# Longer edge and node-number loads, and residual rows turned on TensorE, in a graph attention kernel

## The chip, the cores and the metric

The kernel runs on one core of one Trainium2 chip. The metric is the device time of one execution in microseconds (us). A profile is one execution recorded by the hardware profiler; the span is the time from its first to its last instruction.

## What is computed

A graph has 6250 nodes with 128 features each and 206,250 edges, sorted by destination. With 8 heads of 16 features:

```python
Q, K, V = x @ WQ, x @ WK, x @ WV                        # 6250 x 128
Eh = edge_attr @ WE                                     # 206250 x 128
score = sum over a head of (K[src] * Q[dst] * Eh) / 4   # per edge and head
score = exp(clip(score, -5, 5))
h = segment_sum(V[src] * score, dst) / (segment_sum(score, dst) + 1e-6)
out = layernorm(x + h)
```

All inputs and the output are float32.

## The kernel before, in words

**Tiles and batches.** The edges are cut into 1612 tiles of 128 edges. Four tiles make a batch (the last few batches have two or one), 406 batches in all. Eleven tiles make a group; the edges of a group fall into a window of 128 destination nodes, and three groups cover a block of 128 nodes, with windows shifted by -43, 0 and 43.

**Start.** The transposed node features xT are loaded whole into SBUF (line 96) and stay there. TensorE makes the table of K and V from them (lines 227 to 246), which goes through a staging tile kvst with two buffers to HBM. Meanwhile GpSimd already gathers rows of x for the first 12 batches (XB), which are projected to K and V on the fly (project, lines 322 to 334). From batch 12 on, GpSimd gathers finished K and V rows from the table.

**One batch.** GpSimd issues one indirect gather for each tile (line 311), 128 rows of 1 KB, into a tile kvrows of a pool with GB = 16 buffers. Behind each batch from the twelfth on it executes an iota into a tile that nobody reads (line 319). From batch LOCK = 20 on, the first gather of batch b depends on the expansion of batch b-2 (line 314): the matmul of line 353, which spreads the rows of Q (loaded by load_q, line 278, in windows of 42 nodes in three bf16 parts) over the edges with a one-hot matrix. VectorE builds that matrix, onehotT (line 343), from node numbers relative to the window; these are held in HBM (relD, written by from_window, line 164) and loaded by load_rel (line 285), broadcast to 126 partitions, for RC = 16 tiles at a time in two buffers. TensorE multiplies the edge features by WE (line 357), from loads of CH = 8 tiles (line 295, load_chunk) in EB = 6 buffers. VectorE multiplies the expanded Q by that product (line 364), TensorE turns the result (turn, line 372), VectorE multiplies by the gathered K (stage_b, line 378) and sums per head (line 381), ScalarE takes the exponential (lines 390 and 392), VectorE forms the messages (line 412), and TensorE sums them per window with a one-hot matrix (stage_c, line 430).

**Finishing a block.** ScalarE copies each finished window to SBUF (line 440). When all windows of a block of 128 nodes are there, finish (line 403) adds them up on TensorE with shift matrices, ScalarE copies the sum (line 407), and a layernorm is made in small steps of VectorE between the batches' work (lines 595 to 620). It adds the block's rows of x, which stage_c has had loaded on SP's queue (load_x, line 591), and its result is stored on the same queue (line 620). The last group of all has its windows added straight into its PSUM tile.

**What sets the order.** Up to batch 12 a scheduler of the framework orders the instructions; from then on the order is that in which the loop over batches (line 463) writes them. SP's queue issues, in this order per batch: a store of a finished block, the edge load, the node numbers, the window of Q, and later the rows of Q just computed (line 266). An instruction at the head of a queue that waits holds up all behind it. In the loop, load_chunk(c + 3) is called when the batches of edge load c begin, load_rel one load ahead, load_q three windows ahead. After the loop, a general path runs if the edges were not sorted as assumed (line 521); here it is skipped.

Of the kernel before, what the change touches and what calls it, by code (L numbers as in the profile page):

```python
# [8 lines left out]
F32 = mybir.dt.float32  # L9
# [3 lines left out]
ALU = mybir.AluOpType  # L13
AX = mybir.AxisListType

P = 128
N, E, D, H, DH = 6250, 206250, 128, 8, 16
# [4 lines left out]
LEFT, RIGHT = 43, 128  # L22
XC = LEFT + N + RIGHT
OFF = (-43, 0, 43)
MW = D + H
B = 4
CH = 8
GB = 16
XB = 12
LOCK = XB + 8  # L30
STEP = 2
# [1 line left out]
HEAD = 132  # L33
NG = (NT + G - 1) // G
AHEAD = 2
EB = 6
SLAG = 2
WT = 8
RC = 16
NJ = (NT + WT - 1) // WT  # L40
QW = 42
QP = 3
# [38 lines left out]
def edge_attention(ctx: ExitStack, tc: tile.TileContext, x, xT, srcT, dstT, dstB, dst0, bnd, lo, eaT,  # L81
                   wq, wkv, we, out, kv, qtab, qs, relD):
    nc = tc.nc
# [8 lines left out]
    xT_sb = cp.tile([P, XC], F32, name="xT_sb")  # L92
# [19 lines left out]
    with ExitStack() as fast:  # L112
# [11 lines left out]
        ident = shift[:, P:2 * P]  # L124
# [78 lines left out]

        gp = fast.enter_context(tc.tile_pool(name="gather", bufs=GB))
        ep = fast.enter_context(tc.tile_pool(name="edges", bufs=EB))
        wp = fast.enter_context(tc.tile_pool(name="work", bufs=3))
        sp = fast.enter_context(tc.tile_pool(name="sums", bufs=7))
# [3 lines left out]
        psT = fast.enter_context(tc.tile_pool(name="psT", bufs=1, space=bass.MemoryType.PSUM))  # L211
# [36 lines left out]
        batches = cut_batches()  # L248
        nbat = len(batches)
        manual = []  # L250
        xbs, stores, norms, pending, ready = {}, [], [], [], []


        built, loaded, regs, rels = [], {}, [], {}
# [25 lines left out]
        def load_rel(c):  # L280
            if c in rels or c * RC >= NT:
# [3 lines left out]
            nc.sync.dma_start(rels[c][:, :n], relD.rearrange("j e -> (j e)")[None, c * RC * P:c * RC * P + n]  # L285
                              .to_broadcast([QROWS, n]))

        chunks, aggs, sums, st8, expanded = {}, {}, {}, {}, {}

        def load_chunk(c):  # L290
            if c in chunks or c * CH >= NT:
                return
            n = min(CH, NT - c * CH) * P
            tl = ep.tile([P, CH * P], F32, name="ea")
            nc.sync.dma_start(tl[:, :n], eaT[:, c * CH * P:c * CH * P + n])
            chunks[c] = tl

        def ea_tiles(t, n):

            load_chunk(t // CH)  # L300
            j = t % CH * P
            return chunks[t // CH][:, j:j + n * P]
# [92 lines left out]
        def add_windows(ps, q, stop):  # L395

            parts = [(k, k[0] * P + offset(*k) - q * P)
                     for k in ((q - 1, 2), (q, 0), (q, 1), (q, 2), (q + 1, 0)) if k in sums]
            for i, (k, s) in enumerate(parts):
                nc.tensor.matmul(ps, shift[:, P - s:2 * P - s], sums[k],  # L400
                                 start=i == 0, stop=stop and i == len(parts) - 1)

        def finish(q):
            ps = psT.tile([P, MW], F32, name="finps", tag="oT")
            add_windows(ps, q, True)
            fin = sp.tile([P, MW], F32, name="fin", bufs=2)
            nc.scalar.copy(fin, ps)
            pending.append(layernorm(nc, sp, fin, xbs.pop(q), out, q, stores))

        def messages(b):  # L410
            n, g, oh, m = st8[b]
# [5 lines left out]
        def stage_c(b):  # L417
            n, g, oh, m = st8.pop(b)
            for i in range(n):
                t = batches[b][i]  # L420
                k = group_of(t)
                if k[1] == 0 and k[0] not in xbs:
                    xbs[k[0]] = load_x(nc, sp, x, k[0])
                first, final = k not in aggs, k == group_of(NT - 1)
                if first:
                    aggs[k] = psA.tile([P, MW], F32, name="agg")
                    if final:
                        add_windows(aggs[k], k[0], False)
                last = t == NT - 1 or group_of(t + 1) != k
                nc.tensor.matmul(aggs[k], oh[:, i, :], m[:, i, :],  # L430
                                 start=first and not final, stop=last)
                if last and final:
                    norms.extend(pending)
                    pending.clear()
                    while norms:
                        fill()
                    norms.append(layernorm(nc, sp, aggs.pop(k), xbs.pop(k[0]), out, k[0], stores))
                elif last:
                    tl = sp.tile([P, MW], F32, name="sum")
                    nc.scalar.copy(tl, aggs.pop(k))  # L440
                    sums[k] = tl
                    if k[1] == 0 and k[0] > 0:
                        ready.append(k[0] - 1)
# [19 lines left out]
        for b in range(nbat + 4):  # L463
            if b >= XB and not manual:
                manual.append(fast.enter_context(tc.manual_schedule()))
            held += [(b + SLAG, store) for store in stores]
            stores.clear()
            if held and (held[0][0] <= b or b >= nbat):
                held.pop(0)[1]()
            if b < nbat:  # L470
                load_chunk(batches[b][0] // CH + EB - 3)
                load_rel(batches[b][0] // RC + 1)
                load_q(batches[b][0] // WT + QLOOK)
                g = gathered.pop(b) if b in gathered else gather(b)
                if b == min(XB, nbat - 1):
                    late_loads()
                if b == min(XB + 8, nbat - 1):
                    relative(C0, NT)
                if b == 14:
                    from_window(1)  # L480
                if b == 0:
                    for i in range(AHEAD):
                        stage_0(i)
                if b > 0:
                    turn(b - 1)
                stage_a(b, g)
            elif b == nbat:
                turn(b - 1)
            norms.extend(pending)
            pending.clear()  # L490
            for q in ready:
                finish(q)
            ready.clear()
            if 0 <= b - 2 < nbat:
                stage_b(b - 2)
            if 0 <= b - 3 < nbat:
                messages(b - 3)
            fill()
            if b + AHEAD < nbat:
                stage_0(b + AHEAD)  # L500
            if b < nbat:
                pairs(b)
            if 0 <= b - 2 < nbat:
                weigh(b - 2)
            if 0 <= b - 3 < nbat:
                stage_c(b - 3)
            fill()
            if b < nbat:
                while len(built) < q_built(min(NJ - 1, batches[b][0] // WT + QLOOK + 2)):
                    q_rows(len(built))  # L510
            if b == min(60, nbat):
                count_inside()
            if b == min(80, nbat + 1):
                inside = nc.values_load(cnt_i[0:1, 0:1], min_val=0, max_val=2 * EPAD,
                                        skip_runtime_bounds_check_because="two counts of EPAD edges")
# [72 lines left out]
def load_x(nc, sp, x, q):  # L588
    n = min(P, N - q * P)
    xb = sp.tile([P, D], F32, name="xb", bufs=3)  # L590
    nc.sync.dma_start(xb[:n], x[q * P:q * P + n])
    return xb


def layernorm(nc, sp, agg, xb, out, q, stores):

    n = min(P, N - q * P)
    def new(name, w, bufs=2):
        return sp.tile([P, w], F32, name=name, bufs=bufs)
    rz, h, st, mv, v, y, vh, w = (new(k, f) for k, f in (  # L600
        ("rz", H), ("h", D), ("st", 6), ("mv", 2), ("v", 1), ("y", 1), ("vh", 1), ("w", 1)))
    vec = nc.vector
    yield vec.tensor_scalar(rz[:n], agg[:n, D:], 1e-6, None, op0=ALU.add)
    yield vec.reciprocal(rz[:n], rz[:n])
    yield vec.tensor_tensor(h[:n].rearrange("p (h d) -> p h d", h=H),
                            agg[:n, :D].rearrange("p (h d) -> p h d", h=H),
                            rz[:n, :, None].to_broadcast([n, H, DH]), op=ALU.mult)
    yield vec.tensor_tensor(h[:n], h[:n], xb[:n], op=ALU.add)
    yield vec.bn_stats(st[:n], h[:n])
    yield vec.bn_aggr(mv[:n], st[:n])  # L610

    yield vec.tensor_scalar(v[:n], mv[:n, 1:2], 1e-5, None, op0=ALU.add)
    yield vec.tensor_scalar(y[:n].bitcast(I32), v[:n].bitcast(I32), -0.5, float(0x5F3759DF),
                            op0=ALU.mult, op1=ALU.add)
    yield vec.tensor_scalar(vh[:n], v[:n], -0.5, None, op0=ALU.mult)
    for _ in range(3):
        yield vec.scalar_tensor_tensor(w[:n], y[:n], vh[:n], y[:n], op0=ALU.mult, op1=ALU.mult)
        yield vec.scalar_tensor_tensor(y[:n], w[:n], 1.5, y[:n], op0=ALU.add, op1=ALU.mult)
    yield vec.tensor_scalar(h[:n], h[:n], mv[:n, 0:1], y[:n], op0=ALU.subtract, op1=ALU.mult)
    stores.append(lambda: nc.sync.dma_start(out[q * P:q * P + n], h[:n]))  # L620
# [46 lines left out]
```

## Time and profile before

| | |
|---|---|
| runs | 2202.32, 2204.58 and 2208.21 us, median 2204.58 |
| the profiled execution's own time | 2208.21 us |
| its span | 2206.3 us |
| mean granted TensorE clock | 0.866 |
| busy: POOL, DVE, PE, ACT | 1719.4, 1626.8, 1468.0, 478.9 us |
| moved by DMA | 398.18 MB, 180 GB/s on the mean |
| requests: edges (512 KB), node numbers (504 KB), residual rows (64 KB) | 202, 101 and 49 |

In the profile PE is TensorE, DVE is VectorE, ACT is ScalarE, POOL is GpSimd and SP the engine that issues most transfers; a q behind a name is the engine's queue of instructions. L311 is line 311. The page gives busy times, then groups of instructions with their mean in ns and the idle time before them with what ended it. A timeline row has the start and the duration in us, the instruction, and in brackets the idle time before it and its releaser. A row of waits has the total in us, the number of times and the longest. A row of windows has the stretch and its length, the busy time of PE, PE's weight loads, DVE, ACT and POOL with counts, the granted clock, the busy share of the DMA engines and GB/s.

### The profile page before, as it was taken

The numbers are of one execution on the slowest core, as the hardware profiler recorded it, in microseconds if no ns is written. First come the engines' busy times: TensorE is split into PE (matmuls) and PEld (weight loads), VectorE is DVE, ScalarE is ACT, GpSimd is POOL, SyncE is SP. The second block draws the span as 40 slices with busy tenths as digits, with TensorE's granted clock in tenths as the row PEclk, the third lists the DMA queues.
The fourth block names the chain that finished last, engine by engine and source line by source line (L and its number), as shares of the span: only waits on it lengthen the run. The fifth ranks groups of instructions, "written<-read, shape, count | busy, mean of one in ns | idle before, by whom it ended". The sixth has DMA issues, their size and how long they took to land.

```text
span 2206.3 us, 25324 instructions
## 1 busy us (share of the span) xinstructions
PE 1468.0 (67%) x6880; PEld 1026.4 (47%) x6880; DVE 1626.8 (74%) x3779; ACT 478.9 (22%) x1572; POOL 1719.4 (78%) x2013
## 2 busy tenths in 40 slices
PE   6976666676666666666666666666766666666665
PEld 4754444454444444444444444444444444444443
DVE  3797778677777777777776776777777777777776
ACT  2522222222222221222221221222222211221211
POOL 7737777877777787787777778778778777777876
PEclk9998888878888998888888898998898888887888
DMA  8746555665566556555666556556655566656552
GB/s 283 247 135 203 173 183 160 192 193 163 171 188 193 180 163 199 177 182 161 181 188 181 181 168 201 179 163 191 186 181 163 177 192 181 181 165 200 176 161 78
DMA packets 178486, 398.18 MB, mean 180 GB/s; under 512 B 61757, under 2 KB 87527, under 8 KB 178337
## 3 DMA queue, kind: packets, MB, share of 16 engines
q0 software_dynamic: 76592, 208.18, 31.8%
q1 hardware_dynamic: 100604, 187.38, 27.2%
q8 instruction: 57, 0.93, 0.2%
q10 hardware_dynamic: 1140, 0.93, 0.1%
q14 instruction: 93, 0.75, 0.1%
HBM read 381.54 MB, written 14.81 MB: 180 GB/s over the span
## 4 chain that ended last, share of the span: by engine, by line
POOL 42%; DMA 21%; DVE 15%; issue 14%; PE 7%; POOLq 0%; ACT 0%; DVEq 0%; ACTq 0%; SPq 0%
POOL kvrows L311 39%; DMA kvrows<-kv,src 20%; POOL pause L319 4%; DVE kq L378 4%; DVE sc L381 3%; PE agg L430 2%; DVE msg L412 2%; DVE onehot L339 2%; PE eps L357 2%; DVE onehotT L343 1%; PE kvps L333 1%; PE pps L372 1%; DVE eq L364 1%; DMA kv<-kvst 1%; DVE sc L384 1%
## 5 line engine op out<-in xcount | busy, mean ns | idle before, releaser
L311 POOL DMA_INDIRECT kvrows<-kv,src x1564 | 1487.1, 951 | 453.1 <-issue 384.8
L430 PE MATMUL agg<-msg,onehot 128*128 128x136 f32 x3224 | 542.5, 318 | 605.0 <-DVE msg L412 295.4
L430 PEld LDWEIGHTS agg<-msg,onehot 128*128 128x128 f32 x3224 | 479.3, 218 | 916.7 <-issue 768.9
L378 DVE TENSOR_TENSOR kq<-kvrows,pps 128x512 f32<-128x512 f32 x406 | 276.3, 680 | 472.6 <-DMA kvrows<-kv,src 468.5
L357 PE MATMUL eps<-ea,we_sb 128*128 128x512 f32 (+1 forms) x812 | 487.9, 686 | 0.7 <-ACT kvrows L334 0.7
L372 PE MATMUL pps<-shift,eq 128*128 128x128 f32 x1612 | 310.2, 324 | 98.3 <-DVE eq L364 85.9
L355 ACT COPY qT<-qps 128x512 f32<-128x512 f32 x406 | 236.7, 583 | 587.1 <-PE qps L353 586.8
L372 PEld LDWEIGHTS pps<-shift,eq 128*128 128x128 f32 x1612 | 214.2, 163 | 155.8 <-DVE eq L364 150.0
L364 DVE TENSOR_TENSOR eq<-qT,eps 128x512 f32<-128x512 f32 x406 | 272.4, 671 | 18.9 <-PE eps L357 16.2
L381 DVE TENSOR_REDUCE sc<-kq 128x32 f32<-128x512 f32 x406 | 276.0, 680 | 7.3
L390 ACT ACTIVATE bank<-sc 128x32 f32<-128x32 f32 x406 | 81.8, 201 | 918.5 <-DVE onehot L339 911.8
L412 DVE TENSOR_TENSOR msg<-kvrows,bank 128x512 f32<-128x512 f32 x406 | 274.5, 676 | 5.6 <-ACT bank L390 5.5
L339 DVE TENSOR_TENSOR onehot<-bank,dst_sb 128x512 f32<-128x512 f32 x406 | 275.4, 679 | 0.0
L357 PEld LDWEIGHTS eps<-ea,we_sb 128*128 128x128 f32 x812 | 186.4, 231 | 31.6 <-ACT kvrows L334 3.2
L343 DVE TENSOR_SCALAR onehotT<-relb,node 126x512 bf16<-126x512 bf16 x406 | 192.7, 476 | 6.4 <-DMA relb<-relD 5.7
L319 POOL IOTA pause<- 128x384 int32 x394 | 185.3, 470 | 2.9
L353 PE MATMUL qps<-onehotT,qw 126*128 126x512 bf16 x406 | 183.2, 451 | 0.7 <-ACT qT L355 0.7
L384 DVE TENSOR_SCALAR sc<-sc 128x32 f32<-128x32 f32 x406 | 89.0, 219 | 7.3
L392 ACT ACTIVATE msg<-sc 128x32 f32<-128x32 f32 x406 | 86.5, 213 | 0.0
L400 PEld LDWEIGHTS finps<-sum,shift 128*128 128x128 f32 x478 | 64.5, 195 | 26.1 <-issue 25.9
L400 PE MATMUL finps<-sum,shift 128*128 128x136 f32 x478 | 64.4, 282 | 0.0
L311 POOL DMA_INDIRECT kvrows<-x,src x48 | 46.0, 958 | 16.2 <-issue 14.0
(67 smaller groups left out, 528.5 us busy)
## 6 DMA issues: line engine op xcount, KB each, us to landing
ea<-eaT SPq DMA_DIRECT2D x201, 512.0 KB
relb<-relD SPq DMA_DIRECT2D x100, 504.0 KB
kvrows<-kv,src POOLq DMA_INDIRECT x1564, 2.8
qw<-qs SPq DMA_DIRECT2D x202, 31.5 KB
kv<-kvst SPq DMA_DIRECT2D x12, 512.0 KB
qs<-qst SPq DMA_DIRECT2D x48, 96.0 KB
xb<-x SPq DMA_DIRECT2D x48, 64.0 KB
out<-h SPq DMA_DIRECT2D x48, 64.0 KB
```

What stands on the lines that cost most here:

```text
L311: ins = nc.gpsimd.indirect_dma_start(out=g[:k, i, :f], out_offset=None, in_=rows, in_offset=bass.IndirectOffsetOnAxis(ap=src_col(t)[:k], a ...
L319: nc.gpsimd.iota(pause, pattern=[[1, 3 * P]], base=0, channel_multiplier=0)
L339: nc.vector.tensor_tensor(oh[:, :n], iota_p[:, None, :].to_broadcast([P, n, P]), rel[:, t0:t0 + n, None].to_broadcast([P, n, P]), op=ALU.i ...
L343: nc.vector.tensor_scalar(ohT[:, :n * P], rels[t0 // RC][:, e0:e0 + n * P], node[:QROWS], None, op0=ALU.is_equal)
L355: nc.scalar.copy(qT[:, :n * P], pq[:, :n * P])
L357: nc.tensor.matmul(pe[:, :n * P], we_sb, ea_tiles(t0, n), start=True, stop=True)
L364: nc.vector.tensor_tensor(eq[:, :n * P], qT[:, :n * P], pe[:, :n * P], op=ALU.mult)
L372: nc.tensor.transpose(pp[:, i, :], eq[:, i * P:i * P + P], ident)
L378: nc.vector.tensor_tensor(t1[:, :n], g[:, :n, :D], pp[:, :n], op=ALU.mult)
L381: nc.vector.tensor_reduce(sc[:, :n], t1[:, :n].rearrange("p b (h d) -> p b h d", h=H), axis=AX.X, op=ALU.add)
L412: nc.vector.tensor_tensor(m[:, :n, :D].rearrange("p b (h d) -> p b h d", h=H), g[:, :n, D:].rearrange("p b (h d) -> p b h d", h=H), exp_p[ ...
L430: nc.tensor.matmul(aggs[k], oh[:, i, :], m[:, i, :], start=first and not final, stop=last)
```

## The change

Edge loads hold CH = 16 tiles instead of 8 (1 MB instead of 512 KB), in EB = 3 buffers instead of 6, and load_chunk is called two loads ahead. Node-number loads hold RC = 32 tiles instead of 16 (1008 KB instead of 504 KB), still in two buffers, which takes 8 KB more per partition; the gather pool has GB = 13 buffers instead of 16, which gives 12 KB back. The loads of residual rows go. In their place TensorE turns 128 columns of xT into rows with an identity matrix, beside the window sums in the same PSUM tile, and ScalarE copies both together; for the last group there is a PSUM tile and a copy of its own. The iota behind each batch, the tie to the expansion two batches back, XB and LOCK are the same in both kernels.

```diff
-CH = 8
-GB = 16
+CH = 16
+GB = 13
...
-EB = 6
+EB = 3
...
-RC = 16
+RC = 32
...
-        xbs, stores, norms, pending, ready = {}, [], [], [], []
+        stores, norms, pending, ready = [], [], [], []
...
+        last_x = {}
...
+        def own_rows(ps, q):
+
+            nc.tensor.transpose(ps, xT_sb[:, LEFT + q * P:LEFT + q * P + P], ident)
+
         def finish(q):
-            ps = psT.tile([P, MW], F32, name="finps", tag="oT")
-            add_windows(ps, q, True)
-            fin = sp.tile([P, MW], F32, name="fin", bufs=2)
+            ps = psT.tile([P, MW + D], F32, name="finps", tag="oT")
+            own_rows(ps[:, MW:], q)
+            add_windows(ps[:, :MW], q, True)
+            fin = sp.tile([P, MW + D], F32, name="fin", bufs=2)
             nc.scalar.copy(fin, ps)
-            pending.append(layernorm(nc, sp, fin, xbs.pop(q), out, q, stores))
+            pending.append(layernorm(nc, sp, fin, fin[:, MW:], out, q, stores))
...
-                if k[1] == 0 and k[0] not in xbs:
-                    xbs[k[0]] = load_x(nc, sp, x, k[0])
                 first, final = k not in aggs, k == group_of(NT - 1)
                 if first:
                     aggs[k] = psA.tile([P, MW], F32, name="agg")
                     if final:
+                        px = psT.tile([P, D], F32, name="xps", tag="oT")
+                        own_rows(px, k[0])
+                        xb = last_x.setdefault(0, sp.tile([P, D], F32, name="xb", bufs=1))
+                        nc.scalar.copy(xb, px)
                         add_windows(aggs[k], k[0], False)
...
-                    norms.append(layernorm(nc, sp, aggs.pop(k), xbs.pop(k[0]), out, k[0], stores))
+                    norms.append(layernorm(nc, sp, aggs.pop(k), last_x[0], out, k[0], stores))
...
-                load_chunk(batches[b][0] // CH + EB - 3)
+                load_chunk(batches[b][0] // CH + 2)
...
-    yield vec.tensor_scalar(rz[:n], agg[:n, D:], 1e-6, None, op0=ALU.add)
+    yield vec.tensor_scalar(rz[:n], agg[:n, D:MW], 1e-6, None, op0=ALU.add)
```

## The prediction

> **What bounds the kernel now.** I read the busy times of the page first, then GpSimd's groups, then GpSimd's own timeline, because the busiest engine by share (POOL, 78%) looks as if it had 22% to spare.
>
> ```profile
> PE 1468.0 (67%) x6880; PEld 1026.4 (47%) x6880; DVE 1626.8 (74%) x3779; ACT 478.9 (22%) x1572; POOL 1719.4 (78%) x2013
> ...
> L311 POOL DMA_INDIRECT kvrows<-kv,src x1564 | 1487.1, 951 | 453.1 <-issue 384.8
> ...
> L319 POOL IOTA pause<- 128x384 int32 x394 | 185.3, 470 | 2.9
> ```
>
> The idle column shows that most of what is missing is "issue": a fixed gap behind every gather, not a wait. The timeline of GpSimd shows one batch:
>
> ```profile
> 1002.88 0.47 POOL L319 IOTA pause<- 128x384 int32 x1
> 1003.51 0.95 POOL L311 DMA_INDIRECT kvrows<-kv,src  x1 [0.16 <-issue]
> 1004.76 0.95 POOL L311 DMA_INDIRECT kvrows<-kv,src  x1 [0.30 <-issue]
> ...
> 1008.23 0.54 POOL L319 IOTA pause<- 128x384 int32 x1
> ```
>
> Four gathers of 0.951, three gaps of 0.30, the iota of 0.47 and gaps of 0.01 and 0.16 make 5.34 us. From one batch's first gather to the next, 380 full batches of four tiles take 5.357 us on the mean, 5.34 in the median: GpSimd runs nearly without a hole. The early timeline of the same engine has the one hole that matters:
>
> ```profile
> 106.13 0.47 POOL L319 IOTA pause<- 128x384 int32 x1
> 139.53 0.95 POOL L311 DMA_INDIRECT kvrows<-kv,src  x1 [32.94 <-DVE sc L384]
> ```
>
> This is batch 20, the first that is tied to an expansion of Q (line 314; LOCK is 20). The releaser that is named is wrong: the expansion of batch 18 on TensorE (line 353) starts at 138.63 and takes 0.63, and 0.27 later the gather starts. So the time is a sum of three: 139.53 until batch 20 may start, then 386 batches of gathers to the end of the last one at 2191.67 (2052.1 us), then 14.6 us of tail to 2206.3. An edit counts only if it moves the release of batch 20, GpSimd's rate, or the tail.
>
> **How much room the tie leaves afterwards.** For each batch b, I took the start of its first gather less the start of ScalarE's copy of the expansion of b-2 (line 355), which follows that expansion at once. It is 0.24 us for batch 20 and 2.07 for 21, then grows; from batch 30 on its median is 14.1 us and its least 7.0 (batch 63, behind the counting of batch 60). So GpSimd never waits for the rest of the core, though the rest waits for it:
>
> ```profile
> DVE kq L378 <- DMA kvrows<-kv,src: 468.5, 243, 6.2
> ...
> POOL kvrows L311 <- DVE sc L384: 37.7, 26, 32.9
> ...
> DVE onehotT L343 <- DMA relb<-relD: 5.7, 3, 3.8
> ```
>
> The 468.5 us are VectorE waiting for rows that GpSimd has yet to ask for or that are landing; they are no time to be won. Loads of node numbers were late three times in all, at the start.
>
> **What limits the first 139.5 us.** The windows show a stage of DMA, then TensorE, then VectorE:
>
> ```profile
> 16.00:50.00 34.00, 25.80 (x104) 19.52 (x102) 13.09 (x36) 10.39 (x31) 25.57 (x28) 0.91 0.90 291
> 50.00:65.00 15.00, 10.61 (x36) 6.65 (x37) 8.50 (x14) 5.79 (x12) 11.49 (x12) 0.81 0.85 256
> 65.00:113.00 48.00, 47.95 (x257) 36.34 (x256) 35.26 (x67) 24.87 (x62) 33.13 (x39) 0.99 0.72 224
> 113.00:139.50 26.50, 19.43 (x100) 13.98 (x99) 25.47 (x61) 6.26 (x22) 0.00 (x0) 0.91 0.31 94
> 139.50:2191.70 2052.20, 1352.16 (x6350) 941.24 (x6349) 1532.00 (x3548) 427.52 (x1434) 1637.95 (x1918) 0.86 0.59 178
> ```
>
> From 65 to 113 PE is busy 47.95 of 48, from 113 to 139.5 DVE 25.47 of 26.5: a shift that arrives at 65 goes through to the release. Before that, the table of K and V waits for its own stores (2.82 us at 37.07), which share the queue with the first loads:
>
> ```profile
> 29.27 0.42 SPq L285 DMA_DIRECT2D relb<-relD  x1
> ...
> 37.07 0.65 ACT L238 COPY kvst<-kvacc 128x256 f32<-128x256 f32 x2 [2.82 <-DMA kv<-kvst]
> ...
> 60.03 0.88 DVE L343 TENSOR_SCALAR onehotT<-relb,node 126x512 bf16<-126x512 bf16 x3 [3.79 <-DMA relb<-relD]
> ...
> 62.90 0.47 PE L326 MATMUL xtps<-shift,kvrows 128*128 128x128 f32 x1 [2.39 <-ACT xgT L328]
> ```
>
> **The change, part by part.** Its own execution is 2208.21 us with a span of 2206.3; the median of the runs is 2204.58, and shifts are added to either alike.
>
> 1. Doubled loads at the start: three stand before the last table stores (edge loads at 16.00 and 41.69, node numbers at 29.27). Each gains 504 to 512 KB. At the 291 GB/s of the window 16 to 50, that is 1.75 us each, 5.2 for three: the upper end. The lower end is 0: the stores may slip in between. I take the node numbers whole (1.75; a store issued 0.5 us behind them is the one waited for) and each edge load at 0.55, since 4 to 5 us pass between it and the next store: +2.9.
> 2. The second load of node numbers now is needed at batch 8, not at batch 4. So VectorE's 3.79 at 60.03 go. Behind them TensorE is late for 2.39; what is late next is the projection of the second batch (line 333), so I take the smaller: -2.4, between 0 and -3.8.
> 3. Own rows: 48 transposes in finish and one in the last group. A 128x128 transpose is 0.32 us by the mean of line 372. ScalarE's copy of a finished window takes 0.27 with 136 columns; a copy of 512 (line 355) takes 0.59, so 128 columns more are some 0.11. In the steady part both lie under GpSimd, at ScalarE 22% and PE 67% busy. If that cover were gone, they would cost 49 x (0.32 + 0.11), 21 us. In the VectorE stage before 139.5 there is one finish, 0 to +0.4: I take 0, as VectorE is then at work on the second window of node numbers.
> 4. The 49 loads of residual rows go from SP's queue. Nothing waits for them in the waits; 0.
> 5. Steady loads: the same bytes (less 3 MB of 398) in half as many requests. Edge loads are now asked for two loads ahead (at least 8 batches, 43 us) instead of three short ones (6 batches, 32 us), node numbers at least 6 batches ahead instead of 2. With 3 buffers an edge load waits for the last use of the third last one, and what stands behind it in SP's queue (node numbers, Q's rows, stores) waits too, for about one batch, 5.4 us; Q's rows are asked for 6 batches ahead, 32 us. 0.
> 6. 13 gather buffers: batches 13 to 19 now wait for messages of batches 0 to 6. Those end at 64.3, 71.1, 75.1, 79.3, 85.4, 89.9 and 95.3; the gathers start at 69.35 and every 5.34 us up to 101.42. All are free, by 3.6 us at the least, and a delay would fall into the 32.94 us hole. Later a buffer is 13 batches old, 70 us. 0.
> 7. Tail: one transpose and one copy on the final window's way, +0.2 (0 to +0.6, the transpose with a copy of 0.27).
> 8. GpSimd's rate: its instructions are the same, in the same order. Its holes (5.357 against a least of 5.33, over 386 batches) are 10 us in all; why single gathers are slow is not shown. I take 0, between -10 and +5.
>
> Sum: 2.9 - 2.4 + 0.2 = +0.7, 2208.9 beside the profiled execution and 2205.3 beside the median.
>
> Of the Trainium skill, "DMA: Bandwidth & Descriptors", section "Rules for kernel authors", asks for 1 MiB per DMA, and its fixed cost of about 2 us would, as an estimate for some 200 requests fewer, promise 400 us; the waits above show that nobody stands behind these requests, so I count none of it. The same page, "Queues, rings and completion order", speaks against the change: an engine alternates between queues packet by packet, so longer rows could hold up the gathers' packets; that would be the second rival.
>
> **Rivals.**
> - *The start gets longer* (same side of the bound): item 1 whole, item 2 worth nothing: 5.2 + 0.4 + 0.6 = +6.2, 2210.8. For it: DMA share 0.90 in the window. Against it: the 3.79 us stall is plainly a node-number load. Chance 0.14, a third of it above the bound.
> - *Gathers come too late* (slower): where an edge load and node numbers go out together, 2 MB stand on the queues where 1 MB did. By 291 GB/s that is 3.5 us more. VectorE's product began 1.83 to 9.26 us after a batch's last gather from batch 25 on. The tie bites when a batch is late by more than the room of 7.0 to 14.1 us. If every meeting (51) overshot by 1 us, +51: 2256. Against it: 3.5 is half of the least room. Chance 0.04.
> - *The holes close* (faster): half requests, fewer disturbances of GpSimd: -10 and item 2: 2192. For it: 16 of the periods exceed 5.45 us. Against it: of the 33 gathers over 0.975 us after 130, 19 have no SP request within 1.5 us. Chance 0.07.
> - The change does not do what it says, SP being held elsewhere: no time differs, 2204.6; within the forecast.
>
> **Numbers.** Forecast 2205.3, chance 0.75, its own range 2200 to 2210 (ends of items 1, 2 and 7, with the 2 to 4 us by which the shown runs differ). The whole range takes in the start's rival and a part of the closed holes: 2198 to 2213. The bound of 0.3% is 6.6 us, about what a measurement of this kernel can tell from no change. Faster 0.07, same 0.84, slower 0.09 (0.05 from the start, 0.04 from late gathers).
>
> **What would show it.** In the profile after: GpSimd's periods stay at 5.34 to 5.36; batch 20 starts between 136 and 145; no onehotT waits near 60; the copy into kvst near 37 waits about 2 us longer; the tail stays within a microsecond of 14.6; xb vanishes from the DMA issues. I am wrong if GpSimd waits again after batch 25, if its gathers or gaps change their length, or if the release moves by more than 6 us.

## The result, and the profile after

The changed kernel takes 2221.58 us in the median of 4 runs (2220.18 to 2223.96), the kernel before 2204.11 (2202.32 to 2208.21, 4 runs): ratio 1.0078, 95% interval 1.006 to 1.0095. It is slower by 17.5 us where 0.7 was forecast, and outside the forecast range. Of the runs below, one execution of e1_order took 3532.39 us and is left out of its median.

The profiled execution took 2221.16 us, span 2219.3 (2206.3 before). The prediction's sum of three splits the 13.0 us; the other 4.5 of the median's 17.5 are that the profiled run of before lies 4.1 above its median and that of the changed kernel 0.4 below its own. The release is the start of batch 20's first gather.

| part of the span | before | after | difference | forecast |
|---|---|---|---|---|
| until batch 20 is released | 139.53 | 155.17 | +15.6 | +0.5 |
| from there to the end of the last gather | 2052.1 | 2048.5 | -3.6 | 0 |
| tail | 14.6 | 15.6 | +1.0 | +0.2 |

The page of the changed kernel, in the columns that the prediction read, shows the long part unchanged:

```profile
PE 1456.2 (66%) x6929; PEld 1018.7 (46%) x6929; DVE 1608.3 (72%) x3779; ACT 483.1 (22%) x1573; POOL 1715.5 (77%) x2013
...
L312 POOL DMA_INDIRECT kvrows<-kv,src x1564 | 1482.4, 948 | 469.0 <-issue 379.8
...
L320 POOL IOTA pause<- 128x384 int32 x394 | 185.4, 471 | 2.7
```

A gather takes 948 ns for 951, and the 49 transposes show only as TensorE's count, 6929 for 6880. GpSimd's timeline has the loss, in the same hole as before:

```profile
106.94 0.47 POOL L320 IOTA pause<- 128x384 int32 x1
155.17 0.94 POOL L312 DMA_INDIRECT kvrows<-kv,src  x1 [47.76 <-PE qps L354]
```

47.76 us of idle where the prediction's row has 32.94. What was late in front of it is in the waits of the changed kernel (engine, instruction, releaser: us in all, times, longest):

```profile
DVE kq L379 <- DMA kvrows<-kv,src: 459.0, 168, 8.0
...
POOL kvrows L312 <- PE qps L354: 48.6, 6, 47.8
...
DVE wq L161 <- DMA dB_sb<-dstB: 9.2, 1, 9.2
...
PE eps L358 <- DMA ea<-eaT: 3.9, 1, 3.9
DVE onehotT L344 <- DMA relb<-relD: 2.6, 1, 2.6
```

The last three of these rows name loads that SP issues. The first two of them stand in no row of before, and each occurs **once**: against 459 us of harmless waiting for rows they look like nothing, but they lie ahead of the release, where every microsecond counts.

**The late second half of the destinations (9.2).** VectorE's part of the timeline, about batch 14:

```profile
132.79 0.15 DVE L161 TENSOR_TENSOR wq<-dB_sb,bnd_c 74x1 f32<-74x1 int32 x1 [9.25 <-DMA dB_sb<-dstB]
```

and before, where it did not wait:

```profile
117.30 0.15 DVE L161 TENSOR_TENSOR wq<-dB_sb,bnd_c 74x1 f32<-74x1 int32 x1
```

from_window(1), called at batch 14, turns that half into node numbers. Its load (line 158, 296 KB) is issued by SP, whose timeline reads:

```profile
107.56 0.35 SPq L278 DMA_DIRECT2D qw<-qs  x1
116.63 0.34 SPq L296 DMA_DIRECT2D ea<-eaT  x1
117.17 0.35 SPq L278 DMA_DIRECT2D qw<-qs  x1
117.56 0.37 SPq L189 DMA_DIRECT2D src<-srcT  x1
117.97 0.43 SPq L190 DMA_DIRECT2D dst_sb<-dstT  x1
118.59 0.35 SPq L278 DMA_DIRECT2D qw<-qs  x1
118.99 0.27 SPq L158 DMA_DIRECT2D dB_sb<-dstB  x1
```

and before:

```profile
107.48 0.27 SPq L158 DMA_DIRECT2D dB_sb<-dstB  x1
```

SP issues nothing from 107.9 to 116.63: the edge load there is to go into the oldest of three buffers, which batch 11 still reads. Behind it the queue bursts out: 1 MB of edges, two loads of 740 KB, and last the one that VectorE needs. It goes out at 118.99, 11.5 us later than in the kernel before, and VectorE has it at 132.79. Its place behind that burst costs too: its 74 packets of 4 KB run from 124.96, when the 740 KB loads are nearly through, to 132.39, 13.4 us after its issue; before, the last 4 KB packet ends at 116.41, 8.9 us after its issue. So its last packet comes 16.0 us later, 11.5 by the issue and 4.5 by the longer time from there. The copy of Q's expansion (qT) of batch 15 follows that of batch 14 by 18.1 us:

```profile
124.51 0.58 ACT L356 COPY qT<-qps 128x512 f32<-128x512 f32 x1 [0.80 <-PE qps L354]
...
142.64 0.58 ACT L356 COPY qT<-qps 128x512 f32<-128x512 f32 x1 [2.51 <-PE qps L354]
```

Before, by 8.3, so the difference is +9.8:

```profile
118.34 0.59 ACT L355 COPY qT<-qps 128x512 f32<-128x512 f32 x1 [0.80 <-PE qps L353]
...
126.67 0.59 ACT L355 COPY qT<-qps 128x512 f32<-128x512 f32 x1 [2.04 <-PE qps L353]
```

**Edge load 1 (3.9).** TensorE at batch 4:

```profile
82.10 1.10 PE L358 MATMUL eps<-ea,we_sb 128*128 128x512 f32 x2 [3.92 <-DMA ea<-eaT]
```

At batch 0 the loop asks for load 0 // 16 + 2 = 2. Load 1 (tiles 16 to 31, batches 4 to 7) is asked for by nobody until it is used: SP issues it at 73.24, with loads 0, 2 and 3 in the three buffers, after batch 3 lets load 0's buffer go. Before, six short buffers absorbed such a skip.

The start before that went nearly as forecast: the stall at 60 us is gone, the copy into kvst waits longer, and VectorE waits for the first node numbers:

```profile
39.17 1.34 DVE L344 TENSOR_SCALAR onehotT<-relb,node 126x512 bf16<-126x512 bf16 x4 [2.62 <-DMA relb<-relD]
40.66 0.65 ACT L238 COPY kvst<-kvacc 128x256 f32<-128x256 f32 x2 [4.44 <-DMA kv<-kvst]
```

VectorE's product kq, by batch, carries the sum: batch 3 at 77.6 (76.2 before: +1.4), batch 4 at 87.7 (82.2: +5.5, edge load 1 between them), batch 10 at 114.6 (108.4: +6.2); then the 9.8; the release comes at +15.6.

### The profile page after: what moved, and what is told of

It reads as the page before. It is cut to its first block, busy times and chain, and to the rows that moved or that the text cites. A ratio compares the mean times of both kernels' runs of the same rounds, so it can differ in the third digit from the quotient of the medians.

```text
span 2219.3 us, 25016 instructions
## 1 busy us (share of the span) xinstructions
PE 1456.2 (66%) x6929; PEld 1018.7 (46%) x6929; DVE 1608.3 (72%) x3779; ACT 483.1 (22%) x1573; POOL 1715.5 (77%) x2013
## 4 chain that ended last, share of the span: by engine, by line
POOL 27%; DMA 24%; DVE 21%; issue 14%; PE 8%; ACT 1%; DVEq 0%; POOLq 0%; ACTq 0%
POOL kvrows L312 25%; DMA kvrows<-kv,src 24%; DVE kq L379 5%; DVE sc L382 5%; PE agg L438 4%; DVE msg L418 3%; POOL pause L320 2%; PE eps L358 2%; DVE eq L365 2%; DVE onehot L340 2%; DVE onehotT L344 1%; PE pps L373 1%; DVE sc L385 1%; PE qps L354 1%; PE finps L401 0%
## 5 line engine op out<-in xcount | busy, mean ns | idle before, releaser
L358 PE MATMUL eps<-ea,we_sb 128*128 128x512 f32 (+1 forms) x812 | 477.2, 672 | 3.9 <-DMA ea<-eaT 3.9
L373 PE MATMUL pps<-shift,eq 128*128 128x128 f32 x1612 | 302.7, 318 | 87.9 <-DVE eq L365 76.8
L373 PEld LDWEIGHTS pps<-shift,eq 128*128 128x128 f32 x1612 | 207.8, 160 | 146.7 <-DVE eq L365 138.1
L358 PEld LDWEIGHTS eps<-ea,we_sb 128*128 128x128 f32 x812 | 181.4, 225 | 32.5 <-issue 4.1
L344 DVE TENSOR_SCALAR onehotT<-relb,node 126x512 bf16<-126x512 bf16 x406 | 180.6, 446 | 3.7 <-DMA relb<-relD 2.6
L354 PE MATMUL qps<-onehotT,qw 126*128 126x512 bf16 x406 | 178.7, 440 | 2.1 <-DMA qw<-qs 1.4
L401 PEld LDWEIGHTS finps<-sum,shift 128*128 128x128 f32 x478 | 59.8, 193 | 15.8 <-issue 15.7
```

What stands on the lines that cost most here:

```text
L344: nc.vector.tensor_scalar(ohT[:, :n * P], rels[t0 // RC][:, e0:e0 + n * P], node[:QROWS], None, op0=ALU.is_equal)
L358: nc.tensor.matmul(pe[:, :n * P], we_sb, ea_tiles(t0, n), start=True, stop=True)
L373: nc.tensor.transpose(pp[:, i, :], eq[:, i * P:i * P + P], ident)
```

## The experiments

The theory is the one just told. The main rival: the doubled loads as such (their bytes in the DMA engines, or the own rows on TensorE) cost the time, and the two waits only show where. The numbered chips below differ in pace: the unedited kernel before takes 2202.32 us on chip 0, but 2446 to 2470 on chips 5, 6, 7, 13 and 15 (more at the end). Each ratio is against the kernel before on the same chip, but sizes in microseconds carry over only from chip 0.

### One load at a time, and more buffers (chip 13)

```diff
 # e1_order: edge load 1 ahead of load 2, in the loop
+                if b == 0:
+                    load_chunk(1)
 # e2_window: line 158's load taken out of from_window, issued at batch 12
+                if b == min(XB, nbat - 1):
+                    load_window(1)
 # e3_both: both edits
 # e4_eb4: four edge buffers; node-number loads short again, for the room
-EB = 3
+EB = 4
-RC = 32
+RC = 16
```

> The changed kernel, with edge load 1 asked for before edge load 2 (the call two loads ahead skips load 1, which then finds all three buffers taken). My theory, that the time went into waits behind SP's queue before batch 20 is released: TensorE's wait of 3.92 us for the edge load at 82 goes, batch 20 starts near 151 instead of 155.17, median near 2217.5. Rival one, the doubled bytes fill the DMA engines at the start: the wait only moves, 155, 2221.6. Rival two, late gathers or GpSimd's rate: no change, 2221.6.

> The changed kernel, with the load of the second half of the destinations (line 158, 296 KB) taken out of its place behind the edge load that waits for a buffer, and asked for earlier. My theory: VectorE's wait of 9.25 us at 132.79 goes, batch 20 starts near 146, median near 2212.3. Rival one (bytes): the load lands no earlier relative to the work, or the same bytes cost the same elsewhere: 2221.6. Rival two (gathers, rate): 2221.6.

> The changed kernel with both edits, edge load 1 before 2 and the second half of the destinations earlier. My theory: both waits go, batch 20 starts near 142, median near 2208.3; what is left of the difference to before (some 2 us of release, 1 us of tail, less 3.6 us of GpSimd's rate) lies within the noise of the runs. If the two waits overlap, the gain is less than the sum of the two single edits. Rivals one and two: 2221.6.

> The changed kernel with four edge buffers instead of three and, to make room, node-number loads of 16 tiles again; the order of the requests in the code is as in the changed kernel. My theory, that it is the buffer that holds SP's queue: edge load 1 finds a free buffer and the load at batch 12 doesn't wait, so both waits go; batch 20 starts between 139 and 143, median 2204 to 2209. If the doubled edge bytes are the cause: it stays above 150, 2216 or more.

| kernel | median us | ratio, interval | qT 14 to 15 | release |
|---|---|---|---|---|
| e1_order | 2471.79 | 1.0028, 1.0013 to 1.0043 | 16.5 | 202.44 |
| e2_window | 2467.07 | 0.9999, 0.999 to 1.0009 | 8.7 | 200.53 |
| e3_both | 2464.66 | 0.999, 0.998 to 1.0 | 8.3 | 196.23 |
| e4_eb4 | 2455.66 | 0.9954, 0.9939 to 0.9969 | 8.5 | 195.01 |

The absolute times expected missed, since the chip is another. The step of qT tells the theory from its rival: it falls to 8.3 to 8.7, as before, with the load issued earlier or with a fourth buffer, and stays where neither is done. Either edit takes the load out of the queue's wait and out of the burst behind it at once, so they don't tell these two apart. (The edit writes the earlier load at batch 12; in the trace of e7_both below, SP issues it at 65.53 already.) The waits of e1_order, up to 260 us, still hold the row (7.6 is this load; the other wait is for the destinations' first half, at 11.8 us, and e3_both has it too):

```profile
DVE wq L161 <- DMA dB_sb<-dstB: 10.3, 2, 7.6
```

Between e1_order and e3_both, which differ in that load alone, lie 7.1 us of time and 6.2 of release; between e2_window and e3_both 2.4 and 4.3.

### The changed kernel again, and the edges alone (chip 6)

```diff
 # p1_edges: the kernel before, with
-CH = 8
+CH = 16
-EB = 6
+EB = 3
-                load_chunk(batches[b][0] // CH + EB - 3)
+                load_chunk(batches[b][0] // CH + 2)
 # a2_after: the changed kernel; e5_both: as e3_both
```

> The changed kernel once more, unedited, beside the edited ones, since the chip of the last four runs is another and slower for every kernel (before 2466.93 us), with waits on TensorE that the first chip doesn't show. On a chip like the first: release of batch 20 at 155, 1.006 to 1.0095 of before. On one like the last: GpSimd waits for the tie in the steady part, so a delay of the start counts there too; the two waits (edge load 1, second half of the destinations) are in the trace, and the ratio to before lies above that of the kernel with both edits by 0.4 to 0.8 per cent.

> The changed kernel with both edits (edge load 1 before 2, second half of the destinations earlier), on the same chip as the unedited one. On a chip like the first, my theory: release near 142, ratio to before 0.999 to 1.003. Rivals (bytes, gathers, rate): like the unedited one, 1.006 to 1.009.

> The kernel before with only the edge loads changed: 16 tiles in 3 buffers, two loads ahead. My theory: both waits are there (they come from the three buffers), release of batch 20 at 150 to 155 on a chip like the first, ratio 1.005 to 1.008. If node numbers, residual rows or the gather buffers are the cause instead: 139 to 142, ratio 1.000 to 1.002.

a2_after 2442.24 (0.9986, 0.9975 to 0.9996), e5_both 2440.37 (0.9974, 0.9965 to 0.9984), p1_edges 2454.32 (1.0031, 1.0019 to 1.0044); qT steps 16.3, 8.3 and 18.2. Own rows and long node-number loads are not in p1_edges, and it has the step (and a wait of 9.3 us for that load): long edge loads in three buffers are enough for it; e4_eb4, with long ones in four, had none. But on this chip the changed kernel is not slower than the one before, and the repair, plain in the step, gives 1.9 us. The releases say as much: 200.25 in a2_after, 198.78 in e5_both. The step is 7.9 shorter, but the copy of qT of batch 14 itself comes 6.1 later in e5_both (177.6 for 171.5); why, is not shown.

### What sets the end at that pace (chip 7)

```diff
 # p2_nodes: the kernel before, with
-GB = 16
+GB = 13
-RC = 16
+RC = 32
 # l1_lock: the kernel before, tied from batch 52 on
-LOCK = XB + 8
+LOCK = XB + 40
 # e6_both: as e3_both
```

> The changed kernel with edge load 1 asked for before 2 and the second half of the destinations earlier, once more, to see it on a chip where TensorE's consumers follow it at once as on the first (ScalarE's copy of the expanded Q 0.04 us behind the expansion's end in the median; 0.77 to 1.0 on the two chips of the seven runs so far). On such a chip, my theory: step from the copy of batch 14 to that of batch 15 of 8.3 us instead of 18.1, batch 20 released near 142, ratio 0.999 to 1.003. Rivals: 1.006 to 1.009. On a slow chip: step 8.3, ratio 0.997 to 0.999 as before.

> The kernel before with only the node-number loads of 32 tiles and 13 gather buffers. My theory: neither of the two waits; VectorE's wait of 3.79 us near 60 goes, the first load delays the table by up to 1.75 us; on a chip like the first batch 20 starts at 137 to 141, ratio 0.998 to 1.001. If the gather buffers or the longer rows of node numbers are the cause of the loss: 1.004 or more.

> The kernel before with the tie of the gathers starting at batch 52 instead of batch 20, to test the claim that the release of batch 20 sets the end one to one. My theory: GpSimd's hole of 32.94 us goes, as the 16 buffers are free in time, and all of it shows at the end: median near 2172 on a chip like the first, ratio 0.985. Rival: the rest of the core (VectorE needs about 4 us per batch) or the landing of gathers takes over at once and the end stays: 0.998 to 1.0. On a slow chip, where the tie holds GpSimd anyway, little: 0.995 to 1.0.

e6_both 2465.5 (0.9984, 0.9972 to 0.9995), p2_nodes 2459.08 (0.9953, 0.9935 to 0.9971), l1_lock 2478.37 (1.0037, 1.0023 to 1.0051). l1_lock, in which batch 20 is not tied, started it at 151.86, where e6_both did at 200.12, and ended later all the same: on this chip an earlier start of batch 20 alone is not an earlier end, as the prediction's first rule has it, and my expectation of a gain failed. GpSimd is held by the tie there: in e6_both the first gather follows the copy of qT two batches back within 0.5 us in 145 of 370 batches (30 to 399), in the changed kernel of the first measurement in none. p2_nodes, for which 0.998 to 1.001 was expected, gained. Its gain and the loss of p1_edges may together be why the changed kernel is no slower at this pace: 1.0031 for the edge loads times 0.9953 for the node numbers and gather buffers is 0.998, a rough estimate across two chips, where a2_after measured 0.9986.

### Both repairs, and GpSimd's bound, at the first measurement's pace (chip 0)

```diff
 # e7_both: as e3_both
 # n1_nopause: the kernel before, with
-            if b >= XB:
-                nc.gpsimd.iota(pause, pattern=[[1, 3 * P]], base=0, channel_multiplier=0)
```

> The changed kernel with edge load 1 issued before load 2 and with the load of the destinations' second half (line 158) issued at batch 12 ahead of the queue's long block. Theory (what lengthened the start is these two loads): where the kernel before takes about 2204 us, the release of batch 20 comes back from 155.2 to between 139 and 143, the rest stays at 2048 to 2052, and the time is 2204 to 2210, ratio 1.000 to 1.003. Rival (the doubled loads as such, or the steady part, cost the 17 us): the release stays near 155 or the rest grows, ratio 1.006 to 1.009. Where the kernel before takes 2446 to 2469 us, both say 0.997 to 0.9995, as the same pair of edits gave twice, and only the step from the copy of qT of batch 14 to that of batch 15 tells: 8 to 9 us by the theory, 16 to 18 by the rival.

> The kernel before without the iota behind each batch (386 batches by about 0.47 us of GpSimd). Theory (GpSimd's own pace sets the steady part where the kernel before takes 2204 us): the distance from one batch's first gather to the next one's falls from 5.34 to about 4.9 until the tie holds it, and the time falls by some 30 to 130 us. Rival (the tie to the expansion, that is TensorE and VectorE, is as near a bound): VectorE works 4.0 and TensorE 3.5 us of a batch of 5.34, so less than 30 us comes. Where the kernel before takes 2446 to 2469 us, the tie already holds 100 and more batches: there the theory says that GpSimd's idle grows by what the iota took and the time moves by less than 1%.

e7_both takes 2208.74 us (9 runs) beside 2202.32: 1.0027, 1.0017 to 1.0037. So the two loads were worth 0.5% of the 0.78, some 11 us; this compares two measurements, as the changed kernel was not run again beside it. GpSimd's timeline of e7_both, and VectorE's:

```profile
145.12 0.94 POOL L317 DMA_INDIRECT kvrows<-kv,src  x1 [35.33 <-PE qps L359]
```

```profile
122.74 0.68 DVE L370 TENSOR_TENSOR eq<-qT,eps 128x512 f32<-128x512 f32 x1
123.34 0.15 DVE L166 TENSOR_TENSOR wq<-dB_sb,bnd_c 74x1 f32<-74x1 int32 x1
```

wq follows without a wait, and qT steps by 8.2. The release lies at 145.12, 10 us ahead of the changed kernel's but, against what I expected, 5.6 behind the kernel before. The steady part is 2048.8 us, as in the changed kernel. So what stays is in the start, where the waits for the first node numbers and for the table's stores are longer than in any other trace at this pace:

```profile
41.84 1.28 DVE L349 TENSOR_SCALAR onehotT<-relb,node 126x512 bf16<-126x512 bf16 x4 [4.54 <-DMA relb<-relD]
```

```profile
43.87 0.65 ACT L243 COPY kvst<-kvacc 128x256 f32<-128x256 f32 x2 [6.90 <-DMA kv<-kvst]
```

The copy of qT of batch 0 comes at 62.5. n1_nopause, whose loads are those of before, has it at 55.7 on the same chip: 6.8 us, which I put down to the doubled first loads. In the changed kernel's own trace the difference is 2.9 (57.8 against 54.9), though SP's requests there have the same sizes and order up to 56 us, so this cost varies between executions.

n1_nopause takes 2077.71 us, ratio 0.9435, 0.9419 to 0.9451: the forecast's view of the steady part holds. Its page and timeline:

```profile
L310 POOL DMA_INDIRECT kvrows<-kv,src x1564 | 1484.1, 949 | 512.0 <-issue 360.7
```

```profile
1003.62 0.95 POOL L310 DMA_INDIRECT kvrows<-kv,src  x1 [0.30 <-issue]
1004.87 0.94 POOL L310 DMA_INDIRECT kvrows<-kv,src  x1 [0.30 <-issue]
```

Without the iota the gaps are 0.30 across the batch's edge too: a batch takes 5.015 us for 5.357 (0.47 + 0.01 + 0.16 go, 0.30 comes: 0.34), and 386 times 0.342 is 132. The last gather ends at 2060.40 for 2191.67. The tie still has 4.7 us of room at the least.

### The doubled first loads, and the version the runs point to (chips 5 and 15)

```diff
 # g2_split: e3_both, and the first load of each kind in two halves
+            rel_part(c, 0, n if c else n // 2)
...
+            ea_part(c, 0, n if c else n // 2)
...
                 if b == 0:
+                    ea_part(0, CH * P // 2, CH * P)
                     load_chunk(1)
+                    rel_part(0, RC * P // 2, RC * P)
 # g4_best and h2_best: g2_split without the iota behind each batch
 # g1_window and h1_window: as e2_window; g3_nodes: as p2_nodes
```

> The changed kernel with the load of the destinations' second half alone issued earlier; edge load 1 stays behind load 2. Where the kernel before takes about 2204 us: if that load behind the waiting edge load is worth the 9.7 us that the chain shows, the release of batch 20 goes from 155.2 to 144 to 148 and the ratio from 1.008 to about 1.003 to 1.005; if edge load 1 is the dearer of the two, or its 3.9 us come on top, the ratio stays above 1.005. Where the kernel before takes 2446 to 2469 us: 0.998 to 1.001, and only the step of qT from batch 14 to 15 (8 to 9 us) tells.

> Both loads put right, and the first edge load and the first node-number load of the start cut into two halves, of which the second is issued at batch 0, behind the table's stores. Theory (what is left of 1.0027 is the doubled loads of the start, which stand ahead of the table's stores): VectorE's wait for the node numbers at 39 to 42 us falls from 2.6 to 4.5 us to under 1.5, the copy of qT of batch 0 starts at 55 to 57 in place of 62.5, the release comes to 138 to 142, and where the kernel before takes about 2204 us the ratio is 0.997 to 1.001. Rival (the rest is in the tail or in the steady part): the release stays at 143 to 146 and the ratio at 1.002 to 1.004. Where the kernel before takes 2446 to 2469 us: 0.994 to 0.999 by both.

> The kernel before with node-number loads of 32 tiles and 13 gather buffers alone. Where the kernel before takes about 2204 us: the doubled load at the start costs 2 to 5 us, the stall at 60 us goes, so the release lies at 138 to 143 and the ratio between 0.999 and 1.002; neither of the two late edge and destination loads shows, as edge loads stay 8 tiles with 6 buffers. If the 17 us came from the node numbers, 1.005 and more. Where the kernel before takes 2446 to 2469 us: 0.994 to 0.997, as measured once.

> As the split version, and without the iota behind each batch: the version that should beat both kernels. Where the kernel before takes about 2204 us: the kernel before without the iota gave 0.9435, so 0.940 to 0.946 here. Where the kernel before takes 2446 to 2469 us the tie to the expansion sets the pace of 100 and more batches, and the iota's 0.47 us are hidden in its waits there: 0.98 to 1.0.

> The changed kernel with the load of the destinations' second half alone issued earlier. On a chip where the kernel before takes about 2204 us: the release of batch 20 at 144 to 148 in place of 155.2 and a ratio of 1.003 to 1.005 if that load is the 9.7 us of the chain; 1.006 and more if edge load 1 is worth more than its 3.9 us. On a chip where it takes 2446 to 2469 us: 0.998 to 1.001.

> Both loads put right, the first edge load and the first node-number load cut into halves, and no iota behind each batch. On a chip where the kernel before takes about 2204 us: release of batch 20 at 138 to 142 if the doubled first loads are what is left of the start, at 143 to 146 if not; ratio 0.940 to 0.946, since the kernel before without the iota gave 0.9435. On a chip where it takes 2446 to 2469 us: 0.996 to 0.999.

| kernel, chip | median us | ratio, interval | qT of batch 0 | release |
|---|---|---|---|---|
| g1_window, 5 | 2468.03 | 0.9998, 0.9988 to 1.0007 | 97.0 | 195.07 |
| g2_split, 5 | 2464.84 | 0.9972, 0.9955 to 0.9989 | 95.2 | 192.29 |
| g3_nodes, 5 | 2458.66 | 0.9961, 0.9947 to 0.9975 | 95.5 | 191.27 |
| g4_best, 5 | 2463.59 | 0.9977, 0.9967 to 0.9986 | 94.5 | 193.50 |
| h1_window, 15 | 2438.06 | 0.9964, 0.995 to 0.9978 | 95.8 | 195.30 |
| h2_best, 15 | 2437.30 | 0.9965, 0.9951 to 0.9979 | 92.9 | 189.98 |

With the destinations put right and edge load 1 left behind load 2, the wait for that one load shows as foretold. The waits of h1_window:

```profile
PE eps L363 <- DMA ea<-eaT: 11.3, 1, 11.3
```

In g1_window it is 8.2 us; in e7_both no such row is left. The split takes the kvst copy's wait for the table's stores away or shortens it (7.2 us in g1_window, none in g2_split; 5.7 and 3.7 in h1_window and h2_best) and brings the start forward by 1.9 to 2.9 us, with node-number waits of 3.6 to 3.9 later on in its place: less than half of what I hoped (62.5 to 55 to 57), and at the first pace it was not measured. On chip 5, g4_best without the iota is no faster than g2_split with it, where dropping it from the kernel before gave 5.65% on chip 0. The iota lies in the tie's waits there: from one batch's first gather to the next one's the median falls from 5.35 to 5.07 us, but the mean only from 5.88 to 5.86, and the gathers that follow qT within 0.5 us rise from 141 to 178 of 370.

One warning on small ratios: e2_window, g1_window and h1_window are the same kernel and gave 0.9999, 0.9998 and 0.9964 (the last outside the expected 0.998 to 1.001). The ratio of one kernel moved by 0.35% between chips, so differences of that size mean something only between kernels of one chip.

**The best version** depends on the chip: at the first pace the kernel before without its iota (2077.71) beats both by 5.6% and more; elsewhere short edge loads with long node-number loads (0.9953 on chip 7, 0.9961 on chip 5) and four edge buffers (0.9954 on chip 13) beat the kernel before. g4_best at the first pace was not measured.

## Why the prediction was wrong, point by point

- **What bounds the kernel: right** where the forecast was made. Periods (5.348 for 5.357), gathers and the room of the tie (least 6.98, median 13.1) stayed, the release went straight into the end, and n1_nopause gave 132 us of span where the arithmetic of the gaps gives 131 (386 times 0.34).
- **Item 5 failed**, and with it the forecast. It said that "with 3 buffers an edge load waits for the last use of the third last one, and what stands behind it in SP's queue (node numbers, Q's rows, stores) waits too, for about one batch, 5.4 us", and priced it at 0, by the room of the steady part. The mechanism was right; the list and the place were not. In the queue behind it also stood the load of the second half of the destinations, which exists once, is issued at batch 14 and used at once, in the VectorE stage that the prediction itself had called the road to the release. It went out 11.5 us later, not 5.4, landed 16.0 later and cost 9.8, where item 5 had 0. Issuing it earlier (e2_window) or a fourth buffer (e4_eb4) took the step away each time.
- **Item 5 again:** "edge loads are now asked for two loads ahead" is false for load 1, which the lookahead skips. That is 4 us in the first trace (+1.4 to +5.5). e7_both removed the wait, h1_window and g1_window kept it. The one line of the loop would have told: put b = 0 into it.
- **Items 1 and 2: right in kind, item 1 too small at its upper end.** Net +1.4 at batch 3 was forecast as +0.5; in e7_both the start up to batch 0 is 6.8 longer, above the 5.2 that the bytes of the doubled loads at 291 GB/s allowed (5.4 with a KB of 1024 bytes). What the stores wait for beyond the bytes, no run shows.
- **Item 3 right**: a transpose takes 0.28 us and the longer copy 0.11 more (0.38 for 0.27), 0.32 and 0.11 by the forecast. **Item 6 right**: no gather waited for a buffer. **Item 7**: +1.0 for +0.2, above its range of 0.6. **Item 8**: -3.6, inside -10 to +5, but the profiled run of before was 4.1 us above its median, so the traces don't show that GpSimd's part got shorter at all.
- **The rivals:** late gathers did not come (a gather lands in 2.8 us in the median in both traces), and whether the holes closed can't be told from item 8's -3.6. "The start gets longer" had the right place, the wrong item, and a good third of the size (5.6 us of start where 15.6 came). Its test (wrong "if the release moves by more than 6 us") is what spoke.

Open: how the 11 us divide between the two loads in time (the traces say 9.8 and 4; e2_window at the first pace was not had); what the remaining 6 us of e7_both are, beyond that they stand in the start (release +5.6); why p2_nodes and g3_nodes gain 0.4 to 0.5% on chips 5 and 7; and on chip 6 why batch 14 came 6 us later in e5_both than in a2_after, where on chip 13 one of its two edits gave 7.1 us of time.

## What to carry to other kernels

When buffers get fewer and loads longer, walk the in-order queue load by load through the start, and list everything that is issued behind a load that must wait for a buffer, the loads that occur once above all: a room measured in the steady part says nothing of them. Put the first loop indices into a changed lookahead by hand and see which load nobody asks for. And a wait row with a count of 1 can be the whole result, if it stands before the release that sets the end.

## What was not expected of the hardware

The same kernel takes 2202 to 2204 us on two measurements and 2446 to 2470 on five other chips, with a granted clock of 0.79 to 0.81 for 0.86 to 0.87; gathers have the same length in all traces (947 to 951 ns). There, what follows a matmul often starts long after the matmul's recorded end. The changed kernel on chip 6, at a point of its timeline:

```profile
1002.34 0.38 PE L354 MATMUL qps<-onehotT,qw 126*128 126x512 bf16 x1
...
1006.23 0.59 ACT L356 COPY qT<-qps 128x512 f32<-128x512 f32 x1 [1.24 <-remote]
```

The expansion ends at 1002.72 by the record, and the copy that needs it starts 3.5 later, put down to "remote". Over that trace the delay has a median of 0.77 us and an upper quartile of 4.26 (medians of 0.76 to 1.42 over the traces of these chips); in the first measurement both are 0.04. The start is stretched too: qT of batch 0 comes at 92.9 to 97.6, where the first pace has 54.9 to 62.5. The batches that this delays are the ones in which the tie holds GpSimd: in a2_after the delay has a median of 4.92 us for the expansions whose gather follows qT within 0.5 us (137 of 370), and 0.04 for the others. So in these batches GpSimd's pace no longer sets the time. That ScalarE's copy and GpSimd's gather come late together speaks for an expansion that ends later than its record, in which the end of a matmul is modelled; whether that is so, and why these chips do it, stays open. Dropping the iota gained 5.65% in the kernel before on chip 0, and nothing in the split version on chip 5.
